# Selective scan: where in the order of the work the diagonals of B are made

## The chip, the cores and the metric

The kernel runs on one core of one Trainium2 chip. A core has a matrix engine (TensorE, PE in the profile), a vector engine (VectorE, DVE), an activation engine (ScalarE, ACT), a general engine (GpSimd, POOL) and a queue for transfers (SyncE, SP). Each takes its instructions strictly in the order in which they were written and stops at the first one whose input or whose buffer is not ready. PEld in the profile are the loads of the stationary operand into TensorE; they overlap its products. The metric is the device time of one execution in microseconds (us), the median of several runs.

## The reference

Four layers follow one another on a batch of four images of 56 x 56 tokens with 128 channels, each a residual on a group-normalised input: window attention with an MLP, a selective scan, a deformable convolution, and window attention with an MLP again. The change touches the second layer alone, and of that only its scan:

```python
xs = jnp.stack([x_flat, x_t, jnp.flip(x_flat, 1), jnp.flip(x_t, 1)], axis=1)   # 4 directions
delta = jax.nn.softplus(delta + delta_bias[None, :, None])
def step(h, inp):
    u_i, d_i, b_i, c_i = inp
    dA = jnp.exp(d_i[..., None] * A)
    h = h * dA + (d_i * u_i)[..., None] * b_i[:, None, :]
    y = jnp.einsum('gdn,gn->gd', h, c_i)
    return (h, y)
```

There are 256 inner channels, 16 states each, 3136 steps, and four directions for each image. The step sizes d, the vectors B and C are the same for all four directions; only u changes its order.

## The kernel before, in words

The images are worked one after the other; the scan of an image is `mamba_scan`. One **unit** is one scan instruction (L1119): 128 channels on the partitions, 16 states times one row of 56 steps along it, for one direction. Two halves of the channels (j), two rows (r) and four directions (d) make 16 units, a **pair of rows**, called s; 28 pairs make an image, so 448 units an image and 1792 in all. In this text the **place** of a unit or of any other instruction is its unit number less 16 s: places 0 to 15 belong to the pair that is being scanned.

The order of the work is written out by hand. One loop over the unit number u emits, in this order: the saving of the state of unit u-1 (`save`, ACT, L1123), the products that make the input of unit u+1 (`inputs`, PE, L1101, four matmuls into a tile `dbu`), two decays (`da`, ACT, L1056), the weighing of unit u-1 by C (`weigh`, POOL, L1128), the scan of unit u (`scan`, DVE, L1119), the carried state put into the input of unit u+1 (`inject`, ACT, L1112), the sum over states of unit u-3 (`add_up`, PE, L1137, eight matmuls), and then whatever a plan holds for this u. The plan is a dictionary from unit number to a list of functions, filled by `at(t, f)`; within one unit the functions run in the order in which they were listed. What the plan holds for each pair:

- `chunk` (one for two pairs, 14 an image): `load` brings the rows of B, C and the step sizes in by two transfers (SP, L962 and L964); `high`, `low`, `low2` split the float32 rows into a high and a low part (`xs`: three ACT copies, one POOL subtraction of 40x224, one ACT copy), and `both` writes the two parts to `x2` (two ACT copies, L983 and L984).
- `rows`: for each row r, `b_rows` turns B by two transposes into one PSUM tile `pbt` (PE, L1002), and `b_diag` makes from it two tiles `dgb` of diagonals (DVE, L1008), one in each of the next two units; `c_spread` (PE, L1021, tile `pcb`) and `c_out` (ACT, L1027) spread C over the partitions, in four parts.
- `inputs_of`, once for each half of the channels: four products of u and step size on POOL (`du`, L1051), their split (`dh`: ACT L1061, POOL L1065, ACT L1068), and four times `turn` (PE, L1073, tile `pt`) with `keep` (ACT, L1077), which turn them for the matmuls of `inputs`. These are the turned products of u.
- `back` (PE, L1154, tile `pyb`, 16 matmuls, at places 3 and 6) and `back_add` (DVE, L1159, places 4, 5, 7 and 8), which add the sums of the pair before to the image.

PSUM sets who waits for whom. `dbu` has two tiles, so the input of unit u+1 can be written only when the scan of unit u-1 has ended. The tiles `pbt`, `pt`, `pcb` and `pyb` share two banks: each new one takes a bank that has been given back earlier in the written order, the one given back first where both are free, and its first product waits for the last reader of what lay there. The list in which functions stand within a unit therefore also decides which bank they get.

Before the change, `pbt` of the next pair's rows 0 and 1 is made at places 0 and 9 and its diagonals at places 1, 2, 10 and 11. The turned products of the next pair are made at places 10 to 13, and those of the current pair's second half at places 2 to 5.

Of the kernel before, what the change touches and what calls it, by code (L numbers as in the profile page):

```python
# [78 lines left out]
class _Net:  # L79
# [848 lines left out]
    def mamba_scan(self, b, xa, ya, s1):  # L928
# [10 lines left out]
        with tc.tile_pool(name="ms", bufs=2, reuse_waits="tile") as sb, tc.tile_pool(name="ms_ps", bufs=2, space=PSUM, reuse_waits="tile") as ps, tc.manual_schedule():  # L939
# [9 lines left out]
            def at(t, f, plan=plan):  # L949
                plan.setdefault(t, []).append(f)  # L950
# [4 lines left out]
            def chunk(c):  # L955

                m = made["c", c] = {}
                first = 32 * c

                def load():  # L960
                    m["xd"] = sb.tile([NX, SC], F32, tag="xd", name="xd", bufs=1)
                    nc.sync.dma_start(m["xd"], self.xd_d[b][:, c * SC : (c + 1) * SC])  # L962
                    m["dl"] = sb.tile([P, 2, SC], F32, tag="dl", name="dl")
                    nc.sync.dma_start(m["dl"], self.dl_d[b][:, :, c * SC : (c + 1) * SC])  # L964

                def split(k):
                    return k.rearrange("k (s t) -> k s t", t=TB)

                def high():
                    m["xs"] = sb.tile([NX, SC // TB, 4, TB], F32, tag="xs", name="xs", bufs=1)  # L970
                    m["xh"] = sb.tile([NX, SC], F32R, tag="xh", name="xh", bufs=1)
                    nc.scalar.copy(m["xh"], m["xd"])
                    for g in (0, 2):
                        nc.scalar.copy(m["xs"][:, :, g, :], split(m["xh"].bitcast(F32)))

                def low():
                    nc.gpsimd.tensor_tensor(m["xs"][:, :, 1, :], split(m["xd"]), split(m["xh"].bitcast(F32)), ALU.subtract)

                def low2():
                    nc.scalar.copy(m["xs"][:, :, 3, :], m["xs"][:, :, 1, :])  # L980

                def both():
                    nc.scalar.copy(x2[:NX], m["xd"])  # L983
                    nc.scalar.copy(split(x2[64 : 64 + NX]), m["xs"][:, :, 1, :])  # L984

                at(first - 32, load)
                at(first - 22, high)
                at(first - 20, low)
                at(first - 18, low2)
                at(first - 14, both)  # L990

            def rows(s):

                m = made["r", s] = {}
                first = 16 * s
                src = made["c", s // 2]
                where = (s % 2) * 2 * HW

                def b_rows(r):
                    m["pb"] = bank("pbt")  # L1000
                    for tb in range(2):
                        nc.tensor.transpose(  # L1002
                            m["pb"][:TK, tb * NX : (tb + 1) * NX], src["xs"][:, (s % 2) * 4 + 2 * r + tb].rearrange("k g t -> k (g t)"), self.ident[:NX, :NX]
                        )

                def b_diag(r, tb):
                    t = m[r, tb] = sb.tile([TK, NST, TB], F32R, tag="dgb", name="dgb", bufs=6)
                    nc.vector.tensor_tensor(  # L1008
                        t,
                        m["pb"][:TK, tb * NX + DTR : tb * NX + DTR + NST][:, :, None].to_broadcast([TK, NST, TB]),  # L1010
                        dmask[:, None, :].to_broadcast([TK, NST, TB]),
                        ALU.mult,
                    )

                def c_spread(k):
                    if k == 0:
                        m["cb"] = sb.tile([P, NST, 2 * HW], F32, tag="cb", name="cb")
                    m["pc", k] = bank("pcb")
                    for i in range(4):
                        r = DTR + NST + 4 * k + i  # L1020
                        nc.tensor.matmul(  # L1021
                            m["pc", k][:, i * 2 * HW : (i + 1) * 2 * HW], lhsT=self.ident2[:, r : r + 1].to_broadcast([64 + NX, P]), rhs=x2[:, where : where + 2 * HW],
                            start=True, stop=True,
                        )

                def c_out(k):
                    nc.scalar.copy(m["cb"][:, 4 * k : 4 * k + 4, :].rearrange("p n t -> p (n t)"), m.pop(("pc", k))[:, : 8 * HW])  # L1027

                for r in range(2):
                    t = first - 16 + 9 * r  # L1030
                    at(t, lambda r=r: b_rows(r))
                    for tb in range(2):
                        at(t + 1 + tb, lambda r=r, tb=tb: b_diag(r, tb))
                for k, t in enumerate((-10, -9, -2, -1)):
                    at(first + t + 1, lambda k=k: c_out(k))
                    at(first + t, lambda k=k: c_spread(k))

            def inputs_of(g):

                s, j = divmod(g, 2)  # L1040
                m = made[g] = {}
                first = 8 * g - 15
                src = made["c", s // 2]
                dl = lambda: src["dl"][:, j, (s % 2) * 2 * HW : (s % 2 + 1) * 2 * HW].rearrange("p (r t) -> p r t", t=HW)
                flat = lambda t: t.rearrange("p d s g t -> p (d s) g t")

                def mult(d):
                    if d == 0:
                        made["du", s] = sb.tile([P, 2, 4, 2 * HW], F32, tag="du", name="du", bufs=1)
                    rows = src["dl"][:, :, (s % 2) * 2 * HW : (s % 2 + 1) * 2 * HW].rearrange("p j (r t) -> p j r t", t=HW)  # L1050
                    nc.gpsimd.tensor_tensor(made["du", s][:, :, d, :].rearrange("p j (r t) -> p j r t", t=HW), rows, self.direction(xa, d, 2 * s, 2), ALU.mult)  # L1051

                def decays(n):
                    m["da"] = das[g % 3]
                    for n in (n, n + 1):
                        nc.scalar.activation(m["da"][:, :, n, 2:], dl(), AF.Exp, scale=A[:, j, n : n + 1])  # L1056

                def high():
                    m["dh"] = sb.tile([P, 4, 4, 4, TB], F32R, tag="dh", name="dh", bufs=1)
                    du = made["du", s][:, j].rearrange("p d (s t) -> p (d s) t", t=TB)  # L1060
                    nc.scalar.copy(flat(m["dh"])[:, :, 0:2, :], du[:, :, None, :].to_broadcast([P, 16, 2, TB]))  # L1061

                def low():
                    du = made["du", s][:, j].rearrange("p d (s t) -> p (d s) t", t=TB)
                    nc.gpsimd.tensor_tensor(flat(m["dh"])[:, :, 2, :], du, flat(m["dh"])[:, :, 0, :].bitcast(F32), ALU.subtract)  # L1065

                def low2():
                    nc.scalar.copy(flat(m["dh"])[:, :, 3, :], flat(m["dh"])[:, :, 2, :].bitcast(F32))  # L1068

                def turn(i):  # L1070
                    m["pt", i] = bank("pt")
                    for d in range(4):
                        nc.tensor.transpose(m["pt", i][:TK, d * P : (d + 1) * P], m["dh"][:, d, i].bitcast(F32).rearrange("p g t -> p (g t)"), self.ident)  # L1073

                def keep(i):
                    m["ut", i] = sb.tile([TK, 4, P], F32R, tag="ut", name="ut", bufs=6)
                    nc.scalar.copy(m["ut", i].rearrange("k d c -> k (d c)"), m.pop(("pt", i))[:TK, :])  # L1077

                for d in range(4 * (1 - j)):
                    at(first - 2 + 2 * d, lambda d=d: mult(d))  # L1080
                for i in range(8):
                    at(first + 5 + i, lambda i=i: decays(2 * i), soon)
                at(first + 5, high)
                at(first + 6, low)
                at(first + 8, low2)
                for i in range(4):
                    at(first + 10 + i, lambda i=i: keep(i))
                    at(first + 9 + i, lambda i=i: turn(i))
# [72 lines left out]
            for s in range(HW // 2):  # L1161
                if s % 2 == 0:
                    chunk(s // 2)
                rows(s)
                for g in (2 * s, 2 * s + 1):
                    inputs_of(g)
                for d in range(4):
                    t = 16 * s + 19 + 3 * (d // 2)
                    if d % 2 == 0:
                        at(t, lambda s=s, d=d: back(s, d // 2))  # L1170
                    at(t + 1 + d % 2, lambda s=s, d=d: back_add(s, d))
# [444 lines left out]
```

## Time and profile before

| | |
|---|---|
| median of 3 runs | 12209.72 us (12207.66 to 12214.56) |
| the profiled execution | 12216.06 us, its span 12214.1 us |
| DVE scans, L1119 | 1792 of 2070 ns, 3632.7 us |
| POOL weighing, L1128 | 1792 of 1951 ns, 3447.4 us |
| DVE diagonals, L1008 | 448, median 598 ns |
| idle time of DVE before a scan, ended by ACT's `inject` | 113.1 us, 120 times |
| idle time of PE before `turn`, ended by a diagonal | 165.4 us, 108 times |
| scans of image 0 | 1022.2 to 2032.6 us |

The profile lists for every engine its busy time, and for each group of instructions the mean duration and the idle time of the engine just before, with the instruction that ended it ("<-"). The trace can also be read as a timeline of one engine: start, length, instruction, shapes, count of merged instructions, and in brackets the idle time before it. Two scans that follow one another overlap by some 0.09 us in it, so that a row of n scans is shorter than n durations. The four images have the four stretches of scans that show in the row of DVE; between them lie attention, MLP and the deformable convolution, which the change does not touch.

### The profile page before, as it was taken

How to read it: one execution, taken by the hardware profiler on the slowest of the kernel's cores; microseconds unless marked ns; L12 is line 12 of the kernel's file. 1: busy time of each engine (PE TensorE's matmuls, PEld its weight loads, DVE VectorE, ACT ScalarE, POOL GpSimd, SP SyncE). 2: the span in 40 equal slices, each digit the busy share in tenths (PEclk: the TensorE clock that was granted, in tenths of full speed). 3: DMA queues.
4: the chain of work that ended last, by engine and by line, in shares of the span. 5: the costliest groups of instructions: out<-in, count | busy, mean ns of one | idle time of the engine just before them, and what ended most of it. 6: DMA issues, size and time to landing. Idle time of an engine off the chain costs nothing.

```text
span 12214.1 us, 220022 instructions
## 1 busy us (share of the span) xinstructions
PE 10965.4 (90%) x86844; PEld 7133.3 (58%) x86844; DVE 9389.8 (77%) x12275; ACT 7562.4 (62%) x19326; POOL 9415.0 (77%) x5876
## 2 busy tenths in 40 slices
PE   5998998998799989999889988999978998997799
PEld 3546886553588845454368875545446886553454
DVE  4758997775999967476699986747679998775675
ACT  3667776564577666656467765665646776564366
POOL 1976997596799939669679975957957997597497
PEclk8999999998899999999989999999988999999899
DMA  1000000004300000000520000000051000004200
GB/s 65 1 1 17 5 5 2 1 2 123 97 6 5 3 1 1 12 1 2 146 75 5 5 3 1 2 12 1 1 165 55 5 5 2 1 1 129 81 1 7
DMA packets 145432, 321.07 MB, mean 26 GB/s; under 512 B 17884, under 2 KB 86672, under 8 KB 144144
## 3 DMA queue, kind: packets, MB, share of 16 engines
q0 software_dynamic: 70848, 231.27, 6.6%
q1 hardware_dynamic: 73264, 74.14, 2.0%
q8 instruction: 686, 11.24, 0.4%
q14 instruction: 346, 2.83, 0.1%
q10 hardware_dynamic: 288, 1.59, 0.0%
HBM read 259.03 MB, written 47.90 MB: 25 GB/s over the span
## 4 chain that ended last, share of the span: by engine, by line
PE 56%; DVE 26%; issue 7%; ACT 7%; POOL 2%; SPq 1%; DMA 1%; DVEq 0%; POOLq 0%; ACTq 0%
DVE hs L1119 18%; PE pm L368 15%; PE po L576 10%; PE pst L549 7%; PE pst L540 3%; PE pd L565 2%; DVE dgb L1008 2%; PE pyb L1154 2%; PE pvt L1443 2%; PE pdo L1451 1%; DVE mx L373 1%; DVE ya L1159 1%; SPq L1288 1%; PE pc L819 1%; PE py L714 1%
## 5 line engine op out<-in xcount | busy, mean ns | idle before, releaser
L373 DVE TENSOR_REDUCE mx<-pm 128x1 f32<-128x512 f32 (+7 forms) x6424 | 3377.1, 560 | 998.9 <-PE pm L368 921.5
L560 POOL TENSOR_TENSOR es<-es,e 128x896 f32<-128x896 f32 x1824 | 3765.8, 2092 | 77.2 <-ACT e L550 29.2
L1119 DVE TENSOR_TENSOR_SCAN hs<-da,dbu 128x928 f32<-128x928 f32 x1792 | 3632.7, 2070 | 113.9 <-ACT dbu L1112 113.1
L550 ACT ACTIVATE e<-pst 128x448 f32<-128x448 f32 (+1 forms) x5600 | 2592.0, 548 | 1535.3 <-PE pst L549 1160.4
L1128 POOL TENSOR_TENSOR hs<-hs,cb 128x896 f32<-128x896 f32 x1792 | 3447.4, 1951 | 52.6 <-ACT carry L1123 46.4
L368 PE MATMUL pm<-ks,qs 32*128 32x448 f32 (+5 forms) x12848 | 2966.5, 529 | 104.2 <-DVE mx L373 90.8
L549 PE MATMUL pst<-qs,ks 32*128 32x448 f32 x11200 | 2326.3, 540 | 0.0
L368 PEld LDWEIGHTS pm<-ks,qs 32*128 32x128 f32 x12848 | 1282.1, 187 | 1210.9 <-DVE mx L373 713.5
L1137 PE MATMUL yt<-w_C,hs 128*116 128x128 f32 x14336 | 1867.9, 273 | 8.2 <-POOL hs L1128 8.2
L540 PE MATMUL pst<-nm,sel 32*128 32x448 f32 x5600 | 1667.6, 527 | 6.9 <-DVE nm L394 6.9
L1137 PEld LDWEIGHTS yt<-w_C,hs 128*116 128x116 f32 x14336 | 1568.3, 135 | 14.5 <-POOL hs L1128 10.9
L1101 PE MATMUL dbu<-dgb,ut 112*128 112x224 f32 x7168 | 1252.1, 297 | 165.8 <-DVE hs L1119 164.4
L576 PE MATMUL po<-e,va 128*32 128x448 f32 (+1 forms) x11200 | 1359.9, 554 | 0.0
L1318 POOL DMA_INDIRECT g<-tab,idx x900 | 875.5, 973 | 503.1 <-issue 206.1
L549 PEld LDWEIGHTS pst<-qs,ks 32*128 32x128 f32 x11200 | 1255.3, 187 | 1.5
L1056 ACT ACTIVATE da<-dl,A 128x112 f32<-128x112 f32 x3584 | 1194.3, 382 | 0.1
L1101 PEld LDWEIGHTS dbu<-dgb,ut 112*128 112x128 f32 x7168 | 945.5, 192 | 304.9 <-DVE hs L1119 274.8
L540 PEld LDWEIGHTS pst<-nm,sel 32*128 32x128 f32 x5600 | 711.1, 185 | 165.8 <-issue 147.7
L294 POOL TENSOR_TENSOR pz<-s,m 64x784 f32<-64x784 f32 x128 | 192.0, 1500 | 774.4 <-DVE m L291 769.9
L1073 PE MATMUL pt<-w_C,dh 128*112 128x128 f32 x3584 | 560.6, 280 | 201.0 <-DVE dgb L1008 165.4
L1123 ACT COPY carry<-hs 128x32 f32<-128x32 f32 x1792 | 396.2, 221 | 548.3 <-DVE hs L1119 527.4
L576 PEld LDWEIGHTS po<-e,va 128*32 128x32 f32 (+1 forms) x11200 | 222.7, 108 | 826.3 <-issue 766.5
(227 smaller groups left out, 14360.0 us busy)
## 6 DMA issues: line engine op xcount, KB each, us to landing
g<-tab,idx POOLq DMA_INDIRECT x900, 3.7
tab<-zero SPq DMA_DIRECT2D x4, 3364.0 KB
dl_d<-dl SPq DMA_DIRECT2D x28, 448.0 KB
dl<-dl_d SPq DMA_DIRECT2D x56, 224.0 KB
tab<-gt SPq DMA_DIRECT2D x16, 448.0 KB
out_dram<-x SPq DMA_DIRECT2D x28, 224.0 KB
tab<-gt SPq DMA_DIRECT2D x16, 336.0 KB
w_L<-in_L_dram SPq DMA_DIRECT2D x4, 973.0 KB
```

The costliest lines, as they stand in the source:

```text
L368: nc.tensor.matmul(pm[:, at : at + m], lhsT=qs[head(h), q : q + P], rhs=ks[head(h), keys], start=True, stop=True)
L373: nc.vector.tensor_reduce(mx[:, i, h, n : n + 1], p, AX.X, ALU.max)
L540: nc.tensor.matmul(pst[g, h][:, :CH], lhsT=self.sel[head(h), :], rhs=nm[head(h), part(g // NKB)], start=True, stop=False)
L549: nc.tensor.matmul(t[:, :CH], lhsT=ks[head(h), k * KB : (k + 1) * KB], rhs=qs[head(h), part(qc)], start=False, stop=True)
L550: nc.scalar.activation(es[g, p][:nk, j, :], t[:nk, :CH], AF.Exp, scale=SCALE)
L560: nc.gpsimd.tensor_tensor(s, es[g - 1, p][:nk] if k == 1 else s, es[g, p][:nk], ALU.add)
L576: nc.tensor.matmul(m["po"][head(h), :CH], lhsT=va[:nk, k, head(h)], rhs=src(h)[:nk], start=(k == 0), stop=(k == NKB - 1))
L1056: nc.scalar.activation(m["da"][:, :, n, 2:], dl(), AF.Exp, scale=A[:, j, n : n + 1])
L1101: nc.tensor.matmul(pu[:, 8 * h : 8 * h + 8, 2 + tb * TB : 2 + (tb + 1) * TB], lhsT=made[g]["ut", 2 * r + tb][:, d, :], rhs=made["r", g // ...
L1119: nc.vector.tensor_tensor_scan(flat(pairs[u // 2][:, d % 2]), flat(made[g]["da"][:, r]), flat(banks.pop(u)), 0.0, ALU.mult, ALU.add)
L1128: nc.gpsimd.tensor_tensor(hs, hs, made["r", g // 2]["cb"][:, :, r * HW : (r + 1) * HW], ALU.mult)
L1137: nc.tensor.matmul(sums[q][:YR, e * P : (e + 1) * P], lhsT=hs[:, n, :], rhs=self.ident, start=(n == 0), stop=(n == NST // 2 - 1), is_trans ...
```

## The change: later diagonals, and the splits with them

In the plan, the diagonals move. `b_rows` of row 0 goes from 16 to 7 units ahead of its pair and that of row 1 from 7 to 2 units ahead, each with its diagonals in the two units behind it. In places: `pbt` at 9 and 14, diagonals at 10, 11, 15 and 0. They are also no longer listed by `rows` itself but by a function that it returns and that is called behind `inputs_of`, so that within one unit they come behind `turn` and `keep`. `pbt` of the second row reads `xs` five units later than before, and the split of the next chunk's rows moves five units later too (`high`, `low`, `low2`), and `both` by two. No instruction is added or taken away.

```diff
                 at(first - 32, load)
-                at(first - 22, high)
-                at(first - 20, low)
-                at(first - 18, low2)
-                at(first - 14, both)
+                at(first - 17, high)
+                at(first - 15, low)
+                at(first - 13, low2)
+                at(first - 12, both)
...
-                for r in range(2):
-                    t = first - 16 + 9 * r
-                    at(t, lambda r=r: b_rows(r))
-                    for tb in range(2):
-                        at(t + 1 + tb, lambda r=r, tb=tb: b_diag(r, tb))
+                def diagonals():
+                    for r in range(2):
+                        t = first - 7 + 5 * r
+                        at(t, lambda r=r: b_rows(r))
+                        for tb in range(2):
+                            at(t + 1 + tb, lambda r=r, tb=tb: b_diag(r, tb))
+
                 for k, t in enumerate((-10, -9, -2, -1)):
                     at(first + t + 1, lambda k=k: c_out(k))
                     at(first + t, lambda k=k: c_spread(k))
+                return diagonals
...
-                rows(s)
+                diagonals = rows(s)
                 for g in (2 * s, 2 * s + 1):
                     inputs_of(g)
+                diagonals()
```

## The prediction

> **What bounds the kernel now.** I read the busy time by engine, then the waits of DVE, then the timelines of DVE and PE over one pair of rows. Inside the scans of image 0, by windows (columns: window, its length, busy us and instructions of PE, PEld, DVE, ACT, POOL, granted clock, DMA share, GB/s):
>
> ```profile
> 1040.00:2000.00 960.00, 871.98 (x7315) 807.03 (x7313) 939.34 (x635) 705.40 (x2417) 948.57 (x596) 1.00 0.02 5
> ```
>
> DVE is busy 97.8% and POOL 98.8%. Who of the two leads shows in the waits: DVE's and PE's that matter here, over the whole span:
>
> ```profile
> ACT dbu L1112 <- PE dbu L1101: 517.3, 801, 2.1
> ...
> PE pt L1073 <- DVE dgb L1008: 165.4, 108, 1.5
> ...
> DVE hs L1119 <- ACT dbu L1112: 113.1, 120, 6.9
> ```
>
> DVE's scans wait 113.1 us for `inject`, which waits for PE's `inputs`. So the chain is DVE, with one hole a pair. Its place, by DVE's timeline from place 12 of one pair to place 9 of the next:
>
> ```profile
> 1483.31 11.96 DVE L1119 TENSOR_TENSOR_SCAN hs<-da,dbu 128x928 f32<-128x928 f32 x6
> 1495.19 0.59 DVE L1008 TENSOR_TENSOR dgb<-pbt,w_C 112x448 fp32r<-112x448 f32 x1
> 1495.71 2.07 DVE L1119 TENSOR_TENSOR_SCAN hs<-da,dbu 128x928 f32<-128x928 f32 x1
> 1497.70 0.59 DVE L1008 TENSOR_TENSOR dgb<-pbt,w_C 112x448 fp32r<-112x448 f32 x1
> 1498.22 4.05 DVE L1119 TENSOR_TENSOR_SCAN hs<-da,dbu 128x928 f32<-128x928 f32 x2
> 1502.19 0.36 DVE L1159 TENSOR_TENSOR ya<-ya,pyb 128x224 f32<-128x224 f32 x1
> 1502.47 2.08 DVE L1119 TENSOR_TENSOR_SCAN hs<-da,dbu 128x928 f32<-128x928 f32 x1
> 1504.46 0.55 DVE L1159 TENSOR_TENSOR ya<-ya,pyb 128x224 f32<-128x224 f32 x1
> 1504.93 4.05 DVE L1119 TENSOR_TENSOR_SCAN hs<-da,dbu 128x928 f32<-128x928 f32 x2
> 1508.90 0.35 DVE L1159 TENSOR_TENSOR ya<-ya,pyb 128x224 f32<-128x224 f32 x1
> 1510.04 2.09 DVE L1119 TENSOR_TENSOR_SCAN hs<-da,dbu 128x928 f32<-128x928 f32 x1 [0.78 <-ACT dbu L1112]
> ```
>
> A pair takes 36.20 us (1483.31 to 1519.51). A scan adds 1.98 us, a diagonal 0.52 (1497.70 to 1498.22). The hole lies ahead of scan 8, where PE has had `pyb` (1.87 us) and `pcb` in one unit. The six scans in a row, places 12 to 17, come right behind the 1.53 us that PE loses to a diagonal at place 11, and none of them is late: that loss costs nothing.
>
> The diagonal at place 2 is cover. `inputs` of unit 4 starts when scan 2 ends, then PE does `add_up`, `pyb`, a `pt`, and `inputs` of unit 5; meanwhile DVE does that diagonal, scans 3 and 4 and a `back_add`, and comes out 0.1 us behind. The last pair of an image has no diagonals at places 1 and 2, and there scan 5 (2008.94) has a hole of its own:
>
> ```profile
> 1990.49 17.90 DVE L1119 TENSOR_TENSOR_SCAN hs<-da,dbu 128x928 f32<-128x928 f32 x9
> 2008.31 0.36 DVE L1159 TENSOR_TENSOR ya<-ya,pyb 128x224 f32<-128x224 f32 x1
> 2008.94 2.09 DVE L1119 TENSOR_TENSOR_SCAN hs<-da,dbu 128x928 f32<-128x928 f32 x1 [0.28 <-ACT dbu L1112]
> ```
>
> **The change, part by part.**
>
> *Diagonals off places 1 and 2, onto 15 and 0.* DVE's work stays: four diagonals of 0.52 us a pair. Without a wait the move is free. The one of place 1 is: there `inputs` waits for the scan before (PE idles 0.40 us there), so all shifts alike. The one of place 2 is not. In the shown pair scan 2 ends at 1497.78 (1495.71 + 2.07), and scan 5 starts 4.69 us later. In the last pair scan 2 ends at 2004.43 (seven scans from 1990.49: 6 x 1.98 + 2.07) and scan 5 starts 4.51 us later. So taking away 0.52 us of DVE's work brings scan 5 only 0.18 us nearer; 0.52 - 0.18 = 0.34, call it 0.35 us, is lost a pair. Ends: 0.12 us of slack before scan 5 by the other row (`inject` ends 1502.25, a waiting scan starts 0.10 after, 1502.35 against 1502.47) gives 0.40; the whole 0.52 if scan 8 also keeps its distance to scan 2; 0 if a wait that I don't see covers it. I take 0.35, the same instructions in the same order. 27 pairs an image have a pair after them: 108 x 0.35 = +37.8 us.
>
> *What comes next, scan 8.* Its chain starts at the `back_add` behind scan 5: `turn` at place 5 takes the bank of `pyb`, waits 0.51 us for that `back_add`, and then `inputs` 7, `add_up`, `pyb`, `pcb`, `inputs` 8 follow without a gap. All of it moves with scan 5, so the 0.78 us stay: 0.
>
> *PE's 1.53 us at place 11.* The new list puts `pt` in the bank of the `pt` before, with a wait for `keep` of about 0.4 us (it ends at 1518.34, PE is there at 1517.95). 108 x 1.1 us of PE's time are freed, worth 0 on DVE (the six scans). Lost cover is no matter: nothing is added there. Behind it in PE's queue, `inputs` 13 then waits for scan 11 instead. Ends: 0, and the 0.78 hole of scan 8 if the lag lasted until then; PE waits for DVE again at 1529.55 (0.17 us) and 1531.52 (0.40), so 0.
>
> *New waits.* `pbt` at place 14 holds a bank, so `pcb` at place 15 waits for `c_out` before it: some 0.5 us (1526.90 to 1527.40), as at place 7 now (0.38). Behind it stands `inputs` of unit 17, at 1527.9 and not 1527.57, needed by `inject` only 1 us or more later, since the diagonals of places 15 and 0 hold DVE 1.04 us longer: 0, and 0.3 if those were not there. `pbt` at 14 waits for `keep`, done at 1525.07 before PE is there: 0. `dgb` has six tiles, its readers gone ten units before: 0.
>
> *The splits, 52 chunks behind an image's first.* ACT: `high` 0.37 + 0.66 us from place 10 to 15, `low2` 0.38 from 14 to 3, `both` 0.75 from 2 to 4; POOL: `low` 0.66 from 12 to 1. They leave a stretch without holes, so no gain. At 15 ACT's `save` comes 0.9 us late, but POOL reaches that unit later still. At 3 and 4 ACT waits for PE anyway (0.77 to 0.95 us). On POOL `low` puts four units of weighing and the `du` at place 5 0.6 us back, and `dh` on ACT waits for that `du` (0.60 us now); ACT has 0.61 us to spare before `inject` 8, and POOL, which starts the pair with `weigh` 14, gets the 0.52 us of the diagonals back. PE's `add_up` at place 10 has 0.83 us to spare before `weigh` 7 ends, 0.83 + 0.35 - 0.62 = 0.56 then. So 0; the upper end is the whole 0.66: 52 x 0.66 = 34. SP: the next chunk's transfer waits for `both`, so it goes two units (4 us) later, 27 units ahead of its use: 0; the step sizes queued behind it wait 6.5 us for `da` now, less then.
>
> *The start of an image.* `pbt` of row 0 moves behind two `pcb`, as row 1's is now (1013.73), still ahead of the first `pt` (1015.74). But the second `pt` can't start beside the first; it waits for `keep` (0.59 us, with decays between them a step of 1.04). And `pbt` of row 1 (0.26) with its wait for the last `keep` stands ahead of `inputs` 0. I add the first scan 1.1 us later; ends -1 (1.42 us of PE's wait for `pcb` go) and +2.1 (two such steps). One diagonal falls behind scan 0: 0.52. Four images: +6.4.
>
> **The sum.** 37.8 + 6.4 = +44 us. The profiled execution took 12216.06 us (span 12214.1 and 2.0 around it), 6.3 above the median of the runs shown; it would take 12260, and the median 12209.7 + 44 = 12254.
>
> [...] In the windows' stretch POOL's own waits are 8.2 us, 26 times for `save`, once a pair: it follows DVE and catches up each time, so I go by DVE's holes. [...]
>
> **The rivals.**
> - *A, the forecast*: a new hole at scan 5, +44 us, 12254; with the ends 0.30 and 0.41 a pair and the image's start, 12238 to 12270.
> - *A+, dearer*: scan 8 does not come nearer with scan 5, the full 0.52 a pair (56), the start at +2.6 each (10), and 0.1 a chunk (5): 12281. For it: PE goes from place 3 to 8 almost without a gap. Against: its 0.51 us wait at 1505.06.
> - *B, nothing*: POOL is the bound or scan 5 is covered; only the image's start stays, 12210 to 12216. For it: POOL's 98.8%. Against: the last pair's 0.28 us.
> - *C, faster*: PE's stall at place 11 lags on to scan 8. Then its hole and the 0.09 us of overlap go: 108 x 0.87 = 94 - 6 = 88 us, 12122. It decides if PE still lags when scan 2 ends; at 1531.52 it waits for DVE, so against it.
>
> **How the numbers follow.** About 0.2% (24 us) is what a measurement can tell from no change. A 0.62, A+ 0.12, B 0.13, C 0.13; so slower 0.74, same 0.13, faster 0.13. The time is A's, 12254. The range goes from 12212, within B, to 12284, past A+; outside are C and a part of B.
>
> **What will show it.** A hole of some 0.3 us ahead of scan 5, 108 times, named as ACT's `inject`; the 0.78 ahead of scan 8 unchanged; PE's waits for a diagonal (165.4 us) gone; a pair of 36.55 us; first scans 1 us later. It is wrong if the pair stays at 36.2, if scan 8's hole changes, or if PE begins to wait for POOL.

## The result and the profile after

The changed kernel took 12276.59 us (median of 5 runs, 12256.72 to 12287.91) against 12211.24 us (5 runs, 12207.66 to 12214.56) for the kernel before: a ratio of 1.0050, 95% interval 1.0037 to 1.0064. It is slower by half a per cent; the forecast was 12254 us with a range of 12212 to 12284. The profiled execution took 12276.59 us, its span 12274.8 us, 60.7 us longer than the span before.

DVE's timeline, from scan 12 of one pair to scan 8 of the next, in the changed kernel:

```profile
1048.38 8.01 DVE L1122 TENSOR_TENSOR_SCAN hs<-da,dbu 128x928 f32<-128x928 f32 x4
1056.31 0.59 DVE L1008 TENSOR_TENSOR dgb<-pbt,w_C 112x448 fp32r<-112x448 f32 x1
1056.82 2.07 DVE L1122 TENSOR_TENSOR_SCAN hs<-da,dbu 128x928 f32<-128x928 f32 x1
1058.82 0.59 DVE L1008 TENSOR_TENSOR dgb<-pbt,w_C 112x448 fp32r<-112x448 f32 x1
1059.33 8.01 DVE L1122 TENSOR_TENSOR_SCAN hs<-da,dbu 128x928 f32<-128x928 f32 x4
1067.26 0.36 DVE L1162 TENSOR_TENSOR ya<-ya,pyb 128x224 f32<-128x224 f32 x1
1067.89 2.09 DVE L1122 TENSOR_TENSOR_SCAN hs<-da,dbu 128x928 f32<-128x928 f32 x1 [0.27 <-ACT dbu L1115]
...
1074.34 0.37 DVE L1162 TENSOR_TENSOR ya<-ya,pyb 128x224 f32<-128x224 f32 x1
1075.49 2.09 DVE L1122 TENSOR_TENSOR_SCAN hs<-da,dbu 128x928 f32<-128x928 f32 x1 [0.78 <-ACT dbu L1115]
```

After the diagonal of place 0 come scans 1 to 4 without anything between them, then the `back_add`, and scan 5 waits 0.27 us for `inject`. It starts 0.63 us behind the start of the `back_add` (1067.26 to 1067.89) where it was 0.28 before. The hole ahead of scan 8 is what it was. The list of waits (engine, line, what it waited for; us in total, times, longest) tells the same for the whole span:

```profile
PE pt L1076 <- DVE dgb L1008: 165.4, 108, 1.5
DVE hs L1122 <- ACT dbu L1115: 128.3, 234, 1.1
POOL hs L1131 <- ACT carry L1126: 91.6, 218, 2.1
PEld pcb L1021 <- ACT cb L1027: 85.4, 216, 1.2
```

DVE's scans wait 234 times where it was 120 times. The totals hide where: ahead of scan 5 it is 37.1 us for 2.4 before and ahead of scan 8 83.0 for 83.2, while the first scans of the four images wait 2.3 us for 27.4. PE's wait for a diagonal has not moved by a tenth. POOL waits more often for `save` than before (46.4 us, 126 times then): it follows DVE. `pcb` waits twice a pair for `c_out` (39.6 us, 104 times before).

Most pairs take 36.57 to 36.60 us. But on image 0 every fifth pair, counted by its first `back_add`, took 37.53 and the one behind it 37.05, and so did some of images 2 and 3. With one in the last pair of image 0 that is 13 times in all, each 1.42 us over two ordinary pairs (37.53 + 37.05 - 2 x 36.58). PE's timeline in one of them:

```profile
1095.53 0.71 PE L1104 MATMUL dbu<-dgb,ut 112*128 112x224 f32 x4 [0.58 <-DVE hs L1122]
1096.08 1.04 PE L1140 MATMUL yt<-w_C,hs 128*116 128x128 f32 x8
1098.04 0.99 PE L1104 MATMUL dbu<-dgb,ut 112*128 112x224 f32 x4 [0.92 <-DVE hs L1122]
1098.84 1.91 PE L1140 MATMUL yt<-w_C,hs 128*116 128x128 f32 x8
1100.54 1.06 PE L1076 MATMUL pt<-w_C,dh 128*112 128x128 f32 x4
1101.25 0.90 PE L1104 MATMUL dbu<-dgb,ut 112*128 112x224 f32 x4
1101.99 1.04 PE L1140 MATMUL yt<-w_C,hs 128*116 128x128 f32 x8
```

An `add_up` of 1.04 us takes 1.91 there. By windows of 1 us (columns as in the windows above: window, length, busy us and instructions of PE, PEld, DVE, ACT, POOL, granted clock, DMA share, GB/s):

```profile
1097.20:1098.20 1.00, 0.16 (x1) 0.16 (x2) 1.00 (x2) 0.21 (x3) 1.00 (x2) 1.00 0.00 0
1098.20:1099.20 1.00, 1.00 (x6) 1.00 (x7) 1.00 (x1) 0.74 (x4) 1.00 (x2) 0.55 0.00 0
1099.20:1100.20 1.00, 1.00 (x7) 1.00 (x6) 1.00 (x2) 0.26 (x3) 1.00 (x2) 0.50 0.00 0
1100.20:1101.20 1.00, 1.00 (x7) 1.00 (x6) 1.00 (x1) 0.59 (x3) 1.00 (x1) 0.50 0.00 0
1101.20:1102.20 1.00, 1.00 (x8) 1.00 (x7) 0.74 (x1) 0.01 (x1) 1.00 (x2) 0.75 0.00 0
1102.20:1103.20 1.00, 1.00 (x12) 1.00 (x10) 0.72 (x1) 1.00 (x5) 1.00 (x1) 1.00 0.00 0
```

The granted clock is 0.50 for some 3.4 us, in the very stretch in which PE can afford no lag, and DVE then waits 0.54 us ahead of scan 4 and 0.72 ahead of scan 5. In the first 14 us of an image's scans the granted clock is 0.50 for part of the time, in both kernels. Behind them it was 1.00 throughout in the kernel before. An *event of the clock* is a fall behind those 14 us; the changed kernel has 13.

**Where the time came from.** From the first scan of an image to the end of its last, the four images took 1010.35, 1009.29, 1010.42 and 1009.93 us before, and 1029.20, 1019.49, 1025.98 and 1024.87 after. Image 1 has no event of the clock: +10.2 us, which is the new hole. Four times that is 40.8. The other three are 8.65, 5.36 and 4.74 us above it; that is 18.75 us, and the 13 events at 1.42 make 18.5. So the scans give 40.8 + 18.75 = 59.55, and 1.15 of the 60.7 us lie outside them.

### The profile page after: what moved, and what is told of

It reads as the page before. It is cut to its first block, busy times and chain, and to the rows that moved or that the text cites. A ratio compares the mean times of both kernels' runs of the same rounds, so it can differ in the third digit from the quotient of the medians.

```text
span 12274.8 us, 220032 instructions
## 1 busy us (share of the span) xinstructions
PE 10971.4 (89%) x86844; PEld 7149.3 (58%) x86844; DVE 9405.6 (77%) x12275; ACT 7548.7 (61%) x19326; POOL 9415.2 (77%) x5876
## 4 chain that ended last, share of the span: by engine, by line
PE 62%; DVE 21%; ACT 9%; issue 5%; SPq 1%; POOL 1%; DMA 1%; DVEq 0%; POOLq 0%; ACTq 0%
PE pm L368 15%; DVE hs L1122 13%; PE po L576 10%; PE pst L549 7%; PE pyb L1157 3%; PE pst L540 3%; PE dbu L1104 3%; PE yt L1140 3%; PE pd L565 2%; DVE dgb L1008 2%; PE pt L1076 2%; PE pvt L1447 2%; PE pdo L1455 1%; DVE mx L373 1%; PE pc L819 1%
## 5 line engine op out<-in xcount | busy, mean ns | idle before, releaser
L1131 POOL TENSOR_TENSOR hs<-hs,cb 128x896 f32<-128x896 f32 x1792 | 3448.2, 1944 | 106.0 <-ACT carry L1126 91.6
L1076 PE MATMUL pt<-w_C,dh 128*112 128x128 f32 x3584 | 565.4, 282 | 184.9 <-DVE dgb L1008 165.4
```

Source lines behind the costliest of these rows:

```text
L1131: nc.gpsimd.tensor_tensor(hs, hs, made["r", g // 2]["cb"][:, :, r * HW : (r + 1) * HW], ALU.mult)
```

## The experiments

The chips differ: the kernel before had medians of 12275.66, 12279.16, 12215.16 and 12281.75 us on the four occasions. So ratios are told, each to the kernel before on the same chip; and pairs, which don't differ from chip to chip where the clock is full.

**The change again, on another chip.** No edit.

> The changed kernel once more, unaltered. Two theories on its time. Cover: every pair with a pair after it lasts 36.58 us and not 36.20, because the diagonal at place 2 no longer hides part of PE's work from place 3 on; 108 x 0.38 = 41 us. Clock: some pairs, five apart, last 37.5 us and the one behind 37.05, where the granted TensorE clock drops to about half; 1.41 us each time, 13 times in the profile taken so far, 18 us. Both together give 12255 to 12290, with another number of dropped windows than 13, since they come and go by image. If the clock had no part, the long pairs would sit at the same pairs again and their number would be 13 again.

Measured: ratio 1.0042 (1.0028 to 1.0056). Pairs of 36.58 in all four images and not one event of the clock; first to last scan 1019.4 to 1020.5 us. So the hole is there in both executions, and the events of the clock are not, though the instructions are the same. That doesn't make them a matter of the chip alone: the last section shows what decides whether an execution meets them.

**One part alone: row 1 five places later, without the splits behind the first chunk.** (All later pairs read the first chunk's split rows.)

```diff
-                    t = first - 16 + 9 * r
+                    t = first - 16 + 14 * r
```

> The kernel before with only row 1 moved (tiles of B turned at places 0 and 14, diagonals at 1, 2, 15 and 0). So that the splits need not move, they are left out for every chunk but an image's first, whose rows of B and C are used throughout. Cover theory: the diagonal at place 2 stays, so there is no wait before scan 5; pairs of 36.2 us or up to 0.1 less, and 12195 to 12215 us. Rival, later diagonals cost wherever they are (row 1 behind the turned products): pairs of 36.4 to 36.6 us, some 12235 to 12255.

Measured: ratio 1.0001 (0.9991 to 1.0010), pairs of 36.20. Row 1 from places 10 and 11 to 15 and 0 costs nothing, and nothing is gained by taking the splits away.

**One part taken away: the changed kernel, the splits for the first chunk alone**.

```diff
+                if c == 0:
-                at(first - 17, high)
+                    at(first - 17, high)
...
```

> The changed kernel with the splits left out for every chunk but an image's first (its rows of B and C are used throughout): five ACT instructions and one POOL subtraction less per chunk. Cover theory: the splits are hidden, pairs stay at 36.58 us, time as the changed kernel within what the clock windows make of it (12255 to 12290). Rival, the moved splits hold POOL or ACT up at places 0 to 5: pairs fall to 36.2 to 36.4 us and 20 to 40 us go.

Measured: ratio 1.0051 (1.0034 to 1.0068); pairs of 36.58, with five events of the clock in four images. Without the splits the loss is what it was: the later splits are hidden, as forecast.

**Only row 0's diagonals, only one place.** In the kernel before they go from places 1 and 2 to 0 and 1. Row 1 and the splits stay.

```diff
-                    t = first - 16 + 9 * r
+                    t = first - 17 + 10 * r
```

> The kernel before with one edit: row 0's diagonals one unit earlier, at places 0 and 1 (its `pbt` at place 15); row 1's stay at 10 and 11, the splits stay. Theory (cover: only a diagonal between the ends of scans 2 and 5 hides PE's 4.51 us): a hole of 0.25 to 0.3 us opens ahead of scan 5 as in the changed kernel, pairs of 36.55 to 36.60, first scan to last scan of an image +10 us (1020), ratio 1.003 to 1.004 on 4 images. Rival (the changed kernel lost its time because the row went to the other end of the pair, beside other work of ACT and POOL): pairs of 36.20, ratio 1.000.

Measured: ratio 1.0036 (1.0022 to 1.0049), pairs of 36.58, 1020 us for each image, no event of the clock in any of them. DVE's timeline on image 0:

```profile
1493.89 6.04 DVE L1119 TENSOR_TENSOR_SCAN hs<-da,dbu 128x928 f32<-128x928 f32 x3
1499.84 0.36 DVE L1159 TENSOR_TENSOR ya<-ya,pyb 128x224 f32<-128x224 f32 x1
1500.48 2.09 DVE L1119 TENSOR_TENSOR_SCAN hs<-da,dbu 128x928 f32<-128x928 f32 x1 [0.28 <-ACT dbu L1112]
...
1508.07 2.09 DVE L1119 TENSOR_TENSOR_SCAN hs<-da,dbu 128x928 f32<-128x928 f32 x1 [0.78 <-ACT dbu L1112]
```

Two diagonals, each moved across one scan, reproduce the whole loss but the clock's. At full clock, this is the only part of the change inside the pairs that costs: that no diagonal stands any longer between scan 2 and scan 3.

**The cover put back with other work.** The changed kernel, with two memsets of a spare tile on DVE at place 2:

```diff
+            def more():
+                for _ in range(2):
+                    nc.vector.memset(extra, 0.0)
...
+                at(16 * s + 2, more)
```

> The changed kernel with two memsets of a spare tile (112x224) added on DVE at place 2 of each pair, where the kernel before had a diagonal; nothing reads the tile. A memset of 128x256 took 0.27 us and one of 128x128 0.165, so I expect 0.35 to 0.5 us of DVE's time a pair for the two. Theory (cover): they fill the hole ahead of scan 5, whose 0.27 us of waiting goes, and only what exceeds 0.38 is paid: pairs of 36.58 to 36.70, ratio to the kernel before 1.004 to 1.005. Rival (scan 5's wait moves along with DVE's work, so that any work of DVE counts in full): pairs of 36.95 to 37.1 with the 0.27 us still there, ratio 1.008 to 1.009.

Measured: ratio 1.0054 (1.0040 to 1.0067), pairs of 36.76 to 36.77 but for eight events of the clock in the four images. DVE's timeline:

```profile
1496.98 4.06 DVE L1123 TENSOR_TENSOR_SCAN hs<-da,dbu 128x928 f32<-128x928 f32 x2
1501.04 0.60 DVE L1167 MEMSET extra<- 112x224 f32 x2
1501.56 4.00 DVE L1123 TENSOR_TENSOR_SCAN hs<-da,dbu 128x928 f32<-128x928 f32 x2
1505.48 0.36 DVE L1163 TENSOR_TENSOR ya<-ya,pyb 128x224 f32<-128x224 f32 x1
1505.76 2.08 DVE L1123 TENSOR_TENSOR_SCAN hs<-da,dbu 128x928 f32<-128x928 f32 x1
```

Scan 5 no longer waits. Four scans and the memsets take 8.50 us here (1496.98 to 1505.48), where the four scans alone take 7.93 in the changed kernel (1059.33 to 1067.26): the memsets cost DVE 0.57 us, and the pair grew by 0.19. So 0.38 us of them lay in the hole. That is the size of the loss (36.58 - 36.20), measured by filling it; the ratio of the whole runs is too coarse to add to this. The pair is 0.07 us above the upper end that I expected, since I had put the memsets at 0.35 to 0.5.

**The same idea, tried badly first.** Two products of the spare tile by the mask of the diagonals, at place 2 and, in a second kernel, at place 12:

```diff
+                for _ in range(2):
+                    nc.vector.tensor_tensor(extra, extra, dmask[:, None, :].to_broadcast([TK, 8, TB]), ALU.mult)
...
+                at(16 * s + 2, more)
```

> The changed kernel with two more DVE multiplications of 112x224 in place, on a tile that nothing else reads, behind scan 2 of every pair: some 0.55 us of DVE's time (estimated from the 0.28 to 0.47 us that a back_add of 128x224 adds). Cover theory: DVE waits for PE before scan 5 anyway, so only what is beyond that wait counts, 0.55 - 0.37 = 0.2 us a pair: pairs of 36.75 to 36.8, the wait before scan 5 gone, 112 x 0.2 = 22 us over the changed kernel. Rival, DVE is the bound and each of its instructions counts in full: pairs of 37.1, +62.

> The same two multiplications behind scan 12, in the row of scans that never waits. Cover theory: they count in full, 0.55 us a pair: pairs of 37.1, the wait before scan 5 unchanged, +62 us over the changed kernel, 40 more than at place 2. Rival: as at place 2, whichever of the two it is.

Measured: 1.0457 (1.0440 to 1.0474) and 1.0220 (1.0203 to 1.0237). Neither theory had that: the products themselves were dear. DVE's timeline of the second kernel, in two pairs that follow one another:

```profile
1507.80 0.80 DVE L1168 TENSOR_TENSOR extra<-extra,w_C 112x224 f32<-112x224 f32 x2
...
1526.05 2.09 DVE L1124 TENSOR_TENSOR_SCAN hs<-da,dbu 128x928 f32<-128x928 f32 x1 [0.27 <-ACT dbu L1117]
...
1545.10 2.61 DVE L1168 TENSOR_TENSOR extra<-extra,w_C 112x224 f32<-112x224 f32 x2
```

In the pairs where they took 0.80 us, a pair took 37.30, 0.72 more than 36.58, and scan 5 kept its 0.27: at place 12 the work is paid in full, at place 2 (the memsets) less by 0.38. That much these kernels add. In the others one product took up to nine times the shortest; see the last section. At place 2 scan 5's hole went too, but at the price of 4.75 us of DVE's time a pair in the mean and of 103 events of the clock (32 in the second kernel), so that kernel settles nothing.

**More cover than before: row 0's diagonals at places 2 and 3.** The kernel before with

```diff
-                    t = first - 16 + 9 * r
+                    t = first - 15 + 8 * r
```

> The kernel before with one edit: row 0's diagonals one unit later, at places 2 and 3 (its `pbt` at place 1); all else stays. Theory (cover): there is 1.04 us of diagonals between scans 2 and 5 where 0.52 was nearly enough, so no hole ahead of scan 5; scan 8's chain starts behind the `back_add` of place 5 and comes later with it, so its 0.78 us stay; pairs of 36.20, ratio 0.999 to 1.001. Rival 1 (any move of row 0 costs 0.38 us a pair): 36.58, 1.0035. Rival 2 (PE's lag is one sum from scan 2 to scan 8, and more cover anywhere in it takes from the 0.78): scan 8's wait falls by some 0.4, pairs of 35.8, ratio 0.9965.

Measured: ratio 1.0239 (1.0225 to 1.0253), pairs of 40.08 and 38.45 in the main, 39.3 in the mean of the two: all three expectations missed. PE's timeline, and then DVE's, show what I had left out:

```profile
1488.72 1.04 PE L1137 MATMUL yt<-w_C,hs 128*116 128x128 f32 x8
1491.29 2.04 PE L1154 MATMUL pyb<-w_C,ys 116*128 116x56 f32 x16 [1.53 <-DVE dgb L1008]
1493.12 1.06 PE L1073 MATMUL pt<-w_C,dh 128*112 128x128 f32 x4
1493.84 1.18 PE L1101 MATMUL dbu<-dgb,ut 112*128 112x224 f32 x4
```

```profile
1493.37 0.39 DVE L1159 TENSOR_TENSOR ya<-ya,pyb 128x224 f32<-128x224 f32 x1 [0.23 <-PE pyb L1154]
1495.27 2.09 DVE L1119 TENSOR_TENSOR_SCAN hs<-da,dbu 128x928 f32<-128x928 f32 x1 [1.51 <-ACT dbu L1112]
```

With `pbt` at place 1 and a `pt` at place 2, `pyb` at place 3 gets `pbt`'s bank and waits 1.53 us for the diagonal of place 3, with `inputs` of unit 5 behind it in PE's queue. It is the wait that `pt` has at place 11, of the same length; there it costs nothing, and here scan 5 waits 1.51 us, because here PE has no time to spare. Some of that is the clock's: from about 1493.0 to 1496.5 it is granted at 0.50. A pair with such a fall takes 38.45 us, one with a fall of twice that length 40.08. Seven pairs of the execution have a full clock and take 37.28; scan 5 of one of them:

```profile
1690.30 2.09 DVE L1119 TENSOR_TENSOR_SCAN hs<-da,dbu 128x928 f32<-128x928 f32 x1 [0.72 <-ACT dbu L1112]
```

So at full clock the moved wait costs 1.08 us a pair (37.28 - 36.20), and the rest comes with the clock. What a second diagonal between scans 2 and 5 is worth by itself, this kernel can't tell.

**Work for PE in the changed kernel, at places 0 and 1**, where it waits for scans (0.58 and 0.92 us in the lines above): four transposes of the identity at either place, into a tile that nothing reads. (The tile takes one of the same two banks; two more a pair leave the turn of the others as it was.)

```diff
+            def more():
+                t = bank("more")
+                for i in range(4):
+                    nc.tensor.transpose(t[:, i * P : (i + 1) * P], self.ident, self.ident)
...
+                for t in range(2):
+                    at(16 * s + t, more)
```

> The changed kernel with four more transposes on PE (0.45 us) at place 0 and at place 1 of each pair, into a PSUM tile that nothing reads; PE waits for DVE there by 0.58 and 0.92 us. Clock theory, the drop comes from PE's idle time at places 0 to 2: no pairs of 37.5 us any more, granted clock 1.00 throughout the scans, pairs of 36.58, 12250 to 12262 us, close together. Rival, the drop comes from elsewhere (a phase of the chip, the load of the other engines): the long pairs stay, 12255 to 12290. If the transposes don't fit into the waits, all pairs grow by up to 0.9 us, +97.

Measured: ratio 1.0040 (1.0027 to 1.0053), pairs of 36.58, no event of the clock. Inconclusive on the clock by itself, since the changed kernel without the filler had no event on that chip either; the last section has what the traces add. What it does show is that PE's lag ahead of scan 5 doesn't begin at places 0 and 1: 8 more products a pair there cost nothing, although the first four wait 1.19 us for a diagonal in the bank that they get.

**PE's lag made shorter.** `pyb`'s 16 matmuls are issued as two bursts of 8, at places 3 and 4, 6 and 7. With the burst cut, PE should be ready for scan 5 in time and the place of the diagonals should not matter. The edit, in the kernel before and in the changed kernel:

```diff
-            def back(s, e):
-                pb = made["pb", s, e] = bank("pyb")
-                for d in range(2):
-                    for j in range(2):
+            def back(s, e, d):
+                if d == 0:
+                    made["pb", s, e] = bank("pyb")
+                pb = made["pb", s, e]
+                for j in range(2):
...
-                    if d % 2 == 0:
-                        at(t, lambda s=s, d=d: back(s, d // 2))
+                    at(t + d % 2, lambda s=s, d=d: back(s, d // 2, d % 2))
```

> The kernel before, with each burst of 16 pyb matmuls (1.87 us, places 3 and 6) cut into two of 8, at places 3, 4, 6 and 7, each still ahead of its back_add. Theory, PE's burst is what the scans wait for: the wait before scan 8 (0.87 us with the lost overlap) shrinks to 0.1 and some 0.25 us appear before scan 9, where the second half and pcb meet: pairs of 35.6 to 35.7 us, ratio to before about 0.995 (60 us less; 50 to 94). Rival, the wait before scan 8 belongs to the bank that the turned product at place 5 waits for: pairs of 36.2, ratio 1.

> The changed kernel with the same cut of the pyb bursts. Cover theory: without the long burst PE has the input of scan 5 ready in time, so the diagonal at place 2 covers nothing there; the loss of 0.38 us a pair goes, except that scan 8 has less time behind scan 5 (a wait of about 0.2, and 0.28 before scan 9): pairs of 35.7 to 35.85 us, within 0.2 us of the kernel before with the same cut, ratio to before 0.996 to 0.9975. Rival, the later diagonals cost 0.38 us a pair whatever PE has to do: pairs 0.38 longer than in the kernel before with the cut, 41 us.

Measured: 0.9976 (0.9966 to 0.9986) with the old places of the diagonals, 0.9978 (0.9969 to 0.9988) with the new ones; pairs of 35.62 and 35.95 in turn, and 35.61 and 35.93. The changed kernel with the cut burst, DVE's timeline:

```profile
1482.48 8.02 DVE L1122 TENSOR_TENSOR_SCAN hs<-da,dbu 128x928 f32<-128x928 f32 x4
1490.40 0.36 DVE L1163 TENSOR_TENSOR ya<-ya,pyb 128x224 f32<-128x224 f32 x1
1490.68 2.08 DVE L1122 TENSOR_TENSOR_SCAN hs<-da,dbu 128x928 f32<-128x928 f32 x1
```

The diagonals are gone from place 2 as in the changed kernel, and scan 5 follows the `back_add` after 0.28 us with no wait. (The equal pairs alone would not say it, because POOL is busy 957 of 960 us in both kernels; see below.) So the loss is not the price of the new places; it is the price of PE's unbroken run of work from scan 2's end to `inputs` 5, and it can be paid from either side.

**And what bounds it then.** The kernel before with the cut burst, and the first two `pcb` two units later, away from `pyb`:

```diff
-                for k, t in enumerate((-10, -9, -2, -1)):
+                for k, t in enumerate((-8, -7, -2, -1)):
```

> The kernel before with `pyb`'s 16 matmuls cut into two bursts of 8 a unit apart, as in the earlier run, and the first two `pcb` (places 6 and 7) two units later, at 8 and 9, away from `pyb`. If DVE still set the pace, the 0.51 us left ahead of scan 8 in every second pair would go, pairs of 35.4 to 35.6 and a ratio near 0.995. If POOL has become the bound (its work in a pair is 948.57/960 of 36.20 = 35.77 us, and the cut bursts alone gave pairs of 35.62 and 35.95, 35.79 in the mean), the mean pair stays at 35.7 to 35.8 wherever PE's work stands, the hole only moves, and the ratio stays at 0.997 to 0.998.

Measured: ratio 0.9967 (0.9956 to 0.9978), pairs of 35.45 and 36.08 in turn, 35.77 in the mean. By windows of image 0:

```profile
1040.00:2000.00 960.00, 881.10 (x7416) 820.41 (x7415) 952.00 (x644) 711.42 (x2440) 957.88 (x602) 1.00 0.02 5
```

POOL is busy 99.8%. Moving more of PE's work left the mean pair where the cut burst had put it (35.785), and only the hole wandered. Now POOL is the bound: 948.57 us of work in 960 us of pairs of 36.20 is 35.77 us a pair. This is the fastest kernel of the study, faster than the kernel before and the changed one; the intervals of the three with the cut burst overlap. Of the 43 to 50 us that the scans of these three became shorter (3997.0 us with the new places, which had four events of the clock, 3991 with the old ones and 3990 in the last, in four images, against 4040), the medians show 25 to 43. Some 4.5 of the difference, in the last kernel, are at the images' ends: its last `back_add` ends 9.31 to 9.77 us behind the last scan, where it was 8.51 on three images of the kernel before. The rest was not traced.

## Why the prediction was right, and where it was not

- **What bounds it, and the new hole at scan 5: right.** 0.27 us of waiting named as `inject`, in every pair; pairs of 36.58 for 36.55. The term was 108 x 0.35 = 37.8 us and measured 40.8. The upper end, 0.40, which came from counting the slack of 0.12 us, was as near as the value taken (0.38).
- **The move off place 1 and row 1's move are free: right.** The diagonal at place 1 covers nothing (row 0 at places 0 and 1 gives 36.58), row 1 alone gives 36.20. Taken together with the memsets, the reason is shown, not only the sum.
- **Scan 8's hole stays at 0.78: right**, so A+ falls.
- **POOL as the bound (rival B): wrong for this kernel.** Its waits rose from 46.4 to 91.6 us, its busy time in the window of image 0 fell from 948.57 to 934.44 us in 960. That the busiest engine is the bound holds only for the kernels with the cut burst, where POOL stands at 99.7 to 99.8%.
- **The splits at nothing: right.** The changed kernel without them loses as much.
- **"The new list puts `pt` in the bank of the `pt` before": wrong.** PE's wait at place 11 is 165.4 us, 108 times, as before. The step that failed is that of the 108 x 1.1 us freed, and with it the statement of the text that the bank given back first is taken. `pt` at place 11 still gets the bank of `pbt`, two tiles earlier, and in the experiment at places 2 and 3 `pyb` got that of `pbt`, two tiles earlier again: both go with banks that are taken in turn, whatever stands first in the list of a unit. The step was priced at 0 on DVE, so the sum did not suffer; rival C, whose 88 us hung on the end of that stall, was not tested by this kernel, which still has it.
- **`pcb` at place 15 waits for `c_out`: right**, 85.4 us and 216 times, hidden.
- **The start of an image: too dear.** Forecast +1.1 us each and 6.4 in all. From the memset of the carried state to the first scan it took 17.51 us before and 18.04 after on image 0 (1004.66 to 1022.17, 1003.91 to 1021.95): +0.53. On images 1 to 3 the same stretch even became shorter, by 0.63, 0.62 and 0.33 us (11.22, 11.52 and 11.21 before; 10.59, 10.90 and 10.88 after). The second `pt` did start beside the first, which is the failed rule on banks again.
- **The clock: not in the sum at all.** 18.75 us in the profiled execution. Without it the sum of the profile is 60.7 - 18.75 = 42 us, against a forecast of 44. It is what brought the time from the middle of the range to near its upper end; nothing in the range had been set aside for it, so that it fitted is luck.
- **Slips in the sum, too small to matter.** 4 x (1.1 + 0.52) is 6.5 and not 6.4. Rival A's upper end, 12270, is 5 us more than the terms named for it (0.41 x 108 + 4 x 2.62 = 54.8), and the 0.41 stood as 0.40 before.

So the mechanism and its size were right, two small terms nearly cancel (the hole 3.0 us larger, the starts and the rest 5.2 us smaller), and the whole miss of the profiled execution (12276.59 against 12260) is the clock's. The median missed by 22.6 us; the other 6 are that it was forecast from a median 6.3 us below the profiled execution of the kernel before, and the clock of the other executions was not traced.

## What to carry to other kernels

On the engine that sets the pace, count for each stretch between two waits how long the other engine's run of work is, and what the pacing engine does meanwhile: a small operation there may be free, and moving it out costs as much as it covered (0.38 of its 0.52 us), though no work is added. Look then at the run that needs the cover: cutting PE's bursts in two gained 0.2% and made the order of the diagonals indifferent, with POOL as the next bound. Before shifting a step that takes a buffer in turn, count which later step gets that buffer: the same wait of 1.53 us cost nothing at one place, and at another the pair grew from 36.20 to 37.28 us, and to 40.08 with the falls of the clock that came with it.

## What the runs showed of the hardware that I had not expected

**The granted clock fell inside a busy stretch.** It went from 1.00 to 0.50 for 3.4 us behind a stretch in which PE was busy 56% of the time (1.89 of the 3.40 us ahead of the fall at 1098.3), and came back. On image 0 the falls stood at 1098.3, 1282.6 and 1466.9 us: 184.3 us apart, each costing 1.42.

The traces say more. Their record of the granted clock is a row of stretches at 0.50 or 1.00, 226 in the kernel before and 262 in the changed one; the length of each but the last, which ends with the execution, is a whole multiple of 3.413 us to within 0.002. So a grid of steps of 3.413 us can be laid over each image. The 184.3 us between two falls are 54.0 such steps and five pairs (3 x 36.58 + 37.53 + 37.05); my estimate is that this is why every fifth pair met the same phase. Five profiles have the changed kernel's two waits of PE for scans, 0.58 and 0.92 us, and no products that hold the scans up elsewhere: the changed kernel on both chips, without the splits, with the memsets, and with the cut burst. In these a fall came each time a step ended 0.25 to 0.42 us behind the start of scan 2, 28 times of 28 (in the first of them 13 of 13, at 0.30 to 0.41). At the edge, 0.43 to 0.44, two steps had a fall behind them and two had none, and at no other phase was there one. On the second chip no step ended in that range, which is why it had no event. In five profiles without these two waits (the kernel before, row 1 alone, row 0 at places 0 and 1, and the old places with the cut burst, with and without the moved `pcb`) 25 steps ended there, and neither they nor steps at any other phase had a fall behind them; nor had those of the kernel with the filler for PE, four of which ended there.

So the falls belong to the changed order, and how many of them an execution meets (13, 0, 5, 8 and 4 in these five) depends on how the steps lie to its pairs. What sets off a fall at the end of such a step stays open. Idle time of PE alone does not tell: the 1.53 us at place 11 stand in every pair of the kernel before, without an event, while the same 1.53 us at place 3 went with a fall in nearly every pair.

**The added products on DVE took from 0.36 to 5.3 us.** A product of 112x224, both inputs in SBUF, took 0.36 us at the shortest. In the kernel with them at place 12 the median was 0.39 us and the longest 3.29; in the kernel with them at place 2 the median was 2.01 us and the longest 5.3. POOL, busy 88% of that kernel's scans (843 of 960 us on image 0), ran its products of two inputs beside them, 1.95 us each. DVE's scans, diagonals and `back_add`, which have one input in PSUM, kept their times (2.07, 0.60, and 0.36 or 0.56 us). The median of 2.01 us is near the length of one of POOL's products, and the longest, 5.3 us, is more than two of them; what held the products up was not shown. The memsets of a tile of the same size, which read nothing, took 0.245 us in all 224 records.
